# 52 early gathers, from 24 missing node tiles on, in a two-layer graph attention kernel on one Trainium2 core

## The chip, the cores and the metric

The kernel runs on one core of one Trainium2 chip. The metric is device time in microseconds. Times of engines come from one profiled execution, in which PE is the matrix engine, PEld its weight loads, DVE the vector engine, ACT the scalar engine, POOL the GpSimd engine and SP the engine that issues most plain DMAs. A gather (an indirect DMA: 128 rows of a table in DRAM, picked by 128 indices) is issued by POOL.

## The reference

A graph has N = 6250 nodes with 768 features and E = 100000 edges, sorted by destination, and each node has an edge to itself besides. The reference normalises the features, runs two layers of graph attention and two dense layers, and adds the input. For one attention layer:

```python
h = (x @ W).reshape(n, heads, -1)                  # layer 1: 4 heads of 64; layer 2: 1 head of 256
alpha_s = (h * a_src[None]).sum(-1)
alpha_d = (h * a_dst[None]).sum(-1)
e = jax.nn.leaky_relu(alpha_s[src] + alpha_d[dst], NEG_SLOPE)
m = jax.ops.segment_max(e, dst, num_segments=n)
e = jnp.exp(e - m[dst])
denom = jax.ops.segment_sum(e, dst, num_segments=n)
alpha = e / (denom[dst] + 1e-16)
out = jax.ops.segment_sum(h[src] * alpha[:, :, None], dst, num_segments=n)
return out.reshape(n, -1) + bias
```

The whole is `h = relu(layernorm(x))`, then `relu(gat)` twice, then `relu(h @ Wm1 + bm1) @ Wm2 + bm2`, added to `x`.

## The kernel before

Nodes are worked in NT = 49 tiles of 128, edges in tiles of 128 too. Two edge tiles are a pair, four are a group, and there are NG = 196 groups; a node tile corresponds to four groups in the loop (`t, j = divmod(g, 4)`). A row of layer 1's table holds 268 numbers: 4 heads of 64 features and a one, and 8 exponentials of the source scores.

The node phase (the loop over `i` in NT before L545) loads `x` and its transpose, normalises, multiplies by `W1` on PE, writes row tile `i` to `kept[i]` in SBUF, which stays there, and stores it in `table1` in DRAM (`store1`, L465). Then `layer_edges` runs for layer 1 and again for layer 2. For each group `g` it gathers the source rows of group `g + 8` (`gather`, issued at L641), turns the pairs of group `g` into weighted rows on DVE (`pair`, L708 to L720), and sums them over destinations by a product with a one-hot matrix on PE (`o_ps`, L732). Every second group the sums are taken up (`acc`, L753) and, once a node tile is complete, `node.steps` normalises it, turns it (`tp`, L884) and multiplies by the next weights (`h_ps`, L935). In layer 1 this makes `table2`, in layer 2 the output.

An ordinary gather of layer 1 needs the whole of `table1`. Some pairs are gathered early instead, in the node phase, from the part of the table that is there. `SOON` (L52) lists for each such pair how many node tiles are stored by then (NT minus the number that is missing). Its parts:

- `soon_places` (L331): for each index, whether it lies in the stored part (`soon_ok`), and the index times that (`soon_i`).
- `soon_rows(there)` (L337): called after the store of tile `there - 1`; gathers both tiles of each pair whose time this is, on POOL (L343), into a buffer of the ring `G` (pool `gathered`, 20 buffers of one pair, taken in turn).
- `soon_away` (L347): writes pairs from `G` to DRAM (`soon_d`, on SP, L351), which frees the buffer. In the node phase it does this for pairs that lie `SOON_HELD = 6` tiles back; at the start of layer 1 (L782) for the rest, in the order of their index.
- `soon_back` (L353): when the group's gather would be due, loads the pair from `soon_d` into a new buffer.
- `soon_sources` (L358) and `soon_hits` (L364): spread the pair's source indices over partitions and compare them on DVE with the numbers of the missing nodes, one 128x128 block for each missing tile (L370). The block matrix `soon_hit` has one buffer.
- `soon_missing` (L375): on PE, one product of such a block with `kept[T]` for each missing tile (L380; two records for each). Its PSUM tile shares two buffers with `tp` and `h_ps`.
- `soon_whole` (L383): on DVE, `row * soon_ok + missing` (L387), which completes the rows in `G`.

`SOON_AT` gives pair `i` the place of the second pair of group 8i + 11. One half-pair `k` is completed for each node tile `t`: hits at group 4k, product at 4k + 2, sum at 4k + 5. The order on each engine is that of the program, written out by hand (`manual_schedule`)[...].

Layer 2 has a smaller device of the same sort (`first_rows`, L321, 11 gathers), which is not changed.

Of the kernel before, what the change touches and what calls it, by code (L numbers as in the profile page):

```python
# [27 lines left out]
NT = -(-N // P)  # L28
# [20 lines left out]
THERE = {layer: [there for n, there in stages for _ in range(n)] for layer, stages in EARLY.items()}  # L49


SOON = [NT - m for m in (11, 20, 2, 19, 11, 18, 3, 17, 4, 16, 4, 15, 5, 15, 6, 14, 7, 13, 8, 12, 9, 18,  # L52
                         10)]
SOON_AT = {2 * (8 * i + 11) + 1: i for i in range(len(SOON))}
SOON_FROM, SOON_HELD = min(SOON), 6
BARE = 8


# [2 lines left out]
def kernel(  # L61
# [21 lines left out]
    nc = tc.nc  # L83
# [260 lines left out]
                        out=soon_G[i][:, t], out_offset=None, in_=table[1][:there * P],  # L344
                        in_offset=bass.IndirectOffsetOnAxis(ap=soon_i[:, i, t:t + 1], axis=0))

    def soon_away(there):  # L347

        for i in sorted(soon_G):
            if SOON[i] <= there:  # L350
                nc.sync.dma_start(soon_d[i], soon_G.pop(i).rearrange("p t c -> p (t c)"))  # L351

    def soon_back(i):  # L353
        G = rows_in(1)
# [3 lines left out]
    def soon_sources(pool, i):  # L358

        if i < len(SOON):  # L360
            soon_of[i] = pool.tile([P, 2 * P], I32, name="soon_of", bufs=2)
            nc.sync.dma_start(soon_of[i], bcast(src_rows, 2 * P, 2 * P * soon_pair[i]))

    def soon_hits(pool, k):  # L364

        i, t = divmod(k, 2)
        if i < len(SOON):
            m = NT - SOON[i]
            soon_hit[k] = pool.tile([P, NT - SOON_FROM, P], F32, name="soon_hit")
            nc.vector.tensor_tensor(  # L370
                soon_hit[k][:, :m],
                soon_of[i][:, t * P:(t + 1) * P].unsqueeze(1).to_broadcast([P, m, P]),
                nid_ps[:, SOON[i]:].unsqueeze(2).to_broadcast([P, m, P]), ALU.is_equal)

    def soon_missing(k):  # L375
        if 0 <= k < 2 * len(SOON):
            there, hit = SOON[k // 2], soon_hit.pop(k)
            soon_p[k] = ps.tile([P, TW[1]], F32, name="missing1", tag="n")
            for T in range(there, NT):
                nc.tensor.matmul(soon_p[k], hit[:, T - there], kept[T], start=(T == there),  # L380
                                 stop=(T == NT - 1))

    def soon_whole(G, k):  # L383
        if 0 <= k < 2 * len(SOON):
            i, t = divmod(k, 2)
            row = G[soon_pair[i]][:, t]
            nc.vector.scalar_tensor_tensor(row, row, soon_ok[:, i, t:t + 1], soon_p.pop(k),  # L387
                                           ALU.mult, ALU.add)
# [3 lines left out]
    with tc.tile_pool(name="w1p", bufs=1) as wp, tc.tile_pool(name="x1", bufs=6) as xp, \  # L392
# [107 lines left out]
        for i in range(NT):  # L500
            h = features1(i)
            if i == 0:
                centre(1)
                moments(2)
            elif i == 1:
                centre(2)
                moments(3)
                spread_means(3)
                moments(4)
            else:  # L510
                if i + 3 < NT:
                    moments(i + 3)
                if i + 2 < NT:
                    spread_means(i + 2)
                if i + 1 < NT:
                    centre(i + 1)
            if i == 0:
                fetch_x(6)
                fetch_x(7)
            if i + 8 < NT:  # L520
                fetch_x(i + 8)
            if i + 5 < NT:
                fetch_xT(i + 5)
            if i == 40:
                first_places()
            if 2 <= i < 2 + KI // 2:
                for k in range(2 * i - 4, 2 * i - 2):
                    nc.vector.tensor_reduce(w1[:, k, HID:], score_w[k], AX.X, ALU.add)
            if BARE <= i < 2 * BARE:
                scores1(i - BARE)  # L530
            keep1(i, *h)
            if 4 <= i < BARE + 4:
                halves[i - 4] = halve(heads_row(kept[i - 4])[:, :, :HID // 4])
            if BARE < i <= 2 * BARE:
                store1(i - BARE - 1)
            if BARE < i <= SOON_FROM - 3:
                store1(i - 1)
            if i >= SOON_FROM - 3:
                store1(i)
                soon_rows(i + 1)  # L540
                soon_away(i + 1 - SOON_HELD)
            if i >= 10:
                next(pieces, None)


# [69 lines left out]
    def layer_edges(layer, H, node, pre, matched, pre_pool):  # L615
# [4 lines left out]
        with tc.tile_pool(name=f"eg{layer}", bufs=5) as eg, \  # L620
# [157 lines left out]
            if layer == 1:  # L778
                for r in range(3):
                    fetch_rows(r)  # L780
                soon_sources(pre_pool, 0)
                soon_away(NT)  # L782
                fetch_rows(3)
                for u in range(4):
                    make_mask(u)
# [33 lines left out]
            for g in range(NG):  # L819
                t, j = divmod(g, 4)  # L820
                if layer == 2 and g >= NG - 2:
                    if g == NG - 2:
                        last_pairs()
                    continue
                if g == NG - 2:
                    at_end.append(g)
                gather(g + AHEAD)
                pair(g, 0)
                if g == NG - 1:
                    pair(g, 1)  # L830
                if g == NG - 2:
                    gather_up(NU - 2)
                advance(g)
                if g <= NG - 4:
                    make_hot(g + 1)
                if g in (NG - 4, NG - 3):
                    make_hot(g + 2)
                if j == 0:
                    if layer == 1:
                        fetch_rows(t + 4)  # L840
                        if t % 2:
                            soon_sources(pre_pool, (t + 1) // 2)
                    node.prefetch(t)
                    meet(t + 1)
                    if layer == 1:
                        soon_hits(pre_pool, t)
                elif j == (2 if t < NT - 1 else 1):
                    node.ahead(t)
                    if layer == 1:
                        soon_missing(t)  # L850
                elif j % 2:
                    if layer == 1 and j == 1:
                        soon_whole(G, t - 1)
                    make_mask((g + 7) // 2)
                if g == NG - 3:
                    idle_ps.append(ps.tile([P, 4 * P], F32, name="idle_ps", tag="e"))
                if g >= NG - 3:
                    stay_warm(3)
                if g < NG - 1:
                    pair(g, 1)  # L860
                advance(g)
                if j == 3:
                    join(t + 1)
                if taken_up(g) is not None:
                    gather_up(taken_up(g))
                if NG - 3 <= g < NG - 1:
                    stay_warm(3)
                hot.pop(g, None)
                if layer == 1 and g == NG - 6:
                    first_sources(2)  # L870
# [533 lines left out]
```

## Time and profile before

| | |
|---|---|
| median of 3 runs | 2589.47 us (2586.82 to 2594.48) |
| the profiled execution | 2102.47 us, of which the span is 2100.7 us |
| busy share of the span | PE 80%, PEld 58%, DVE 67%, ACT 20%, POOL 73% |
| mean granted clock of PE | 0.884 |
| gathers | 1507 at L641, 46 at L343, 11 at L321 |
| products of the missing rows (L380) | 1028 records, 249.1 us of PE |
| their one-hot rows (L370) | 46, 75.3 us of DVE |
| writes to `soon_d` | 23 of 268.0 KB, 6.9 us to landing in the median |
| loads from `soon_d` | 23 of 268.0 KB, 4.0 us |

The profiled execution is 487 us shorter than the median of the runs; the page gives no reason. A line of the page's groups reads: line, engine, operation, output from input, count, busy time, mean in ns of one, and the idle time just before them with what ended it. POOL's busy time does not hold the time in which it issues; PE's ends are modelled.

Three stages follow one another: the node phase to about 165 us, layer 1 to about 1097 us, layer 2 to the end. The stages differ in what fills them, so shares over the whole span say little.

### The profile page before, as it was taken

To read this page: it belongs to the slowest core of one execution; us is meant where nothing else is said; L and a number is where in the kernel's file an instruction comes from. 1 tells how busy PE (TensorE), PEld (TensorE's weight loads), DVE (VectorE), ACT (ScalarE), POOL (GpSimd) and SP (SyncE) were. 2 spreads that over 40 slices of the span, in tenths; PEclk is the share of its full clock that TensorE was granted. 3 is DMA by queue.
4 is the path that set the end of the run, shared out by engine and by line. 5 is a ranking of instruction groups with operands and counts; after the bars stand their busy time and mean duration, and the time that the engine had idled before them with its cause. 6 is when DMAs were issued, how large, how long until landed. Compare 5 with 4: busy or idle time off the path is not lost. (4 is left out here: it accounts for less than half of the span.)

```text
span 2100.7 us, 26499 instructions
## 1 busy us (share of the span) xinstructions
PE 1673.7 (80%) x7728; PEld 1215.5 (58%) x7729; DVE 1411.3 (67%) x4195; ACT 409.8 (20%) x1273; POOL 1523.7 (73%) x1666
## 2 busy tenths in 40 slices
PE   8986879877888888888878777777778777777787
PEld 6864657656665666666645545545455454554554
DVE  7856888878888787888866655555555555555554
ACT  5751111111111111111111111111111111111121
POOL 7057777777777777777777777777777777777774
PEclk9997999989988999999988788888888888888889
DMA  9998666666666666666557455555555555656554
GB/s 343 349 360 290 176 186 181 184 182 186 186 176 183 188 185 178 185 183 187 163 140 225 131 182 170 169 181 160 178 181 158 182 170 168 182 156 182 180 153 123
DMA packets 167328, 400.37 MB, mean 191 GB/s; under 512 B 36631, under 2 KB 54254, under 8 KB 167174
## 3 DMA queue, kind: packets, MB, share of 16 engines
q0 software_dynamic: 75072, 211.10, 38.6%
q1 hardware_dynamic: 90732, 185.99, 24.9%
q10 hardware_dynamic: 1370, 1.48, 0.3%
q8 instruction: 65, 1.06, 0.2%
q14 instruction: 89, 0.73, 0.1%
HBM read 333.87 MB, written 64.56 MB: 190 GB/s over the span
## 5 line engine op out<-in xcount | busy, mean ns | idle before, releaser
L641 POOL DMA_INDIRECT G<-table,src_i x1507 | 1431.2, 950 | 459.7 <-issue 334.5
L732 PE MATMUL o_ps<-G,hw 128*128 128x258 f32 x1564 | 468.9, 438 | 227.3 <-DVE hw L715 226.6
L732 PE MATMUL o_ps<-hw,hot 128*128 128x260 f32 x1564 | 456.7, 434 | 160.4 <-DVE hw L720 135.8
L732 PEld LDWEIGHTS o_ps<-G,hw 128*128 128x128 f32 x1564 | 320.7, 217 | 347.8 <-DVE hw L715 278.5
L708 DVE TENSOR_TENSOR e_ps<-G,e_ps 128x8 f32<-128x8 f32 (+1 forms) x782 | 129.1, 165 | 521.5 <-DMA G<-table,src_i 518.2
L732 PEld LDWEIGHTS o_ps<-hw,hot 128*128 128x128 f32 x1564 | 308.7, 209 | 278.7 <-DVE hw L720 197.6
L762 ACT ACTIVATE sum<-acc 32x260 f32<-32x260 f32 (+1 forms) x384 | 160.0, 417 | 1397.6 <-DVE acc L753 1336.9
L715 DVE TENSOR_SCALAR hw<-iota_ps,dcol,w 128x128 f32<-128x128 f32 x782 | 284.9, 406 | 14.5
L720 DVE TENSOR_TENSOR hw<-G,e_ps 128x520 f32<-128x520 f32 x391 | 271.8, 695 | 13.4
L380 PE MATMUL missing<-kept,soon_hit 128*128 128x268 f32 x1028 | 249.1, 400 | 0.0
L380 PEld LDWEIGHTS missing<-kept,soon_hit 128*128 128x128 f32 x1028 | 199.7, 198 | 36.6
L1058 PE MATMUL y_ps<-wm,mT 128*128 128x384 f32 x392 | 203.3, 654 | 0.3 <-ACT mT L1053 0.3
L438 PE MATMUL h_ps<-w,r 128*128 128x264 f32 (+1 forms) x588 | 139.5, 391 | 11.4 <-ACT r L428 11.2
L669 DVE TENSOR_TENSOR hot<-iota_ps,dcol 128x512 f32<-128x512 f32 x196 | 133.4, 681 | 0.0
L438 PEld LDWEIGHTS h_ps<-w,r 128*128 128x128 f32 x588 | 108.8, 192 | 34.8 <-ACT r L428 15.8
L1058 PEld LDWEIGHTS y_ps<-wm,mT 128*128 128x128 f32 x392 | 86.5, 245 | 64.7 <-issue 39.8
L343 POOL DMA_INDIRECT G<-table,soon_i x46 | 44.1, 960 | 81.0 <-DMA xTt<-in_xT 54.3
L753 DVE SCALAR_TENSOR_TENSOR acc<-acc,keep,o_ps 128x260 f32<-128x260 f32 (+1 forms) x192 | 91.2, 475 | 0.3 <-PE o_ps L732 0.3
L370 DVE TENSOR_TENSOR soon_hit<-soon_of,iota_ps 128x1408 f32<-128x1408 int32 (+18 forms) x46 | 75.3, 1636 | 14.8 <-PE missing L380 14.6
L718 DVE TENSOR_TENSOR e_ps<-e_ps,G 128x8 f32<-128x8 f32 x391 | 68.2, 174 | 13.6 <-DVE e_ps L708 0.2
L711 DVE TENSOR_TENSOR w<-e_ps,G 128x2 f32<-128x2 f32 x391 | 62.3, 159 | 14.3 <-DVE e_ps L708 1.1
L426 DVE TENSOR_TENSOR cent<-xTt,mean_ps 128x768 f32<-128x768 f32 x49 | 46.5, 949 | 33.6 <-DMA xTt<-in_xT 15.8
(415 smaller groups left out, 1172.5 us busy)
## 6 DMA issues: line engine op xcount, KB each, us to landing
xt<-in_x SPq DMA_DIRECT2D x96, 384.0 KB, 6.5
drow<-dmod_d SPq DMA_DIRECT2D x49, 512.0 KB, 5.8
mask_d<-mask SPq DMA_DIRECT2D x97, 256.0 KB, 2.2
mask<-mask_d SPq DMA_DIRECT2D x97, 256.0 KB, 4.4
G<-table,src_i POOLq DMA_INDIRECT x1507, 3.3
xTt<-in_xT SPq DMA_DIRECT2D x49, 384.0 KB, 7.6
out<-y SPq DMA_DIRECT2D x48, 384.0 KB, 3.3
table<-kept SPq DMA_DIRECT2D x49, 134.0 KB, 5.3
```

The source lines that it names most:

```text
L370: nc.vector.tensor_tensor(soon_hit[k][:, :m], soon_of[i][:, t * P:(t + 1) * P].unsqueeze(1).to_broadcast([P, m, P]), nid_ps[:, SOON[i]:].u ...
L380: nc.tensor.matmul(soon_p[k], hit[:, T - there], kept[T], start=(T == there), stop=(T == NT - 1))
L438: nc.tensor.matmul(h_ps[:, :n], r[:, k], w1[:, k, :n], start=(k == 0), stop=(k == KI - 1))
L641: nc.gpsimd.indirect_dma_start(out=G[k // 2][:, k % 2], out_offset=None, in_=table[layer], in_offset=bass.IndirectOffsetOnAxis(ap=src_i[:, ...
L669: nc.vector.tensor_tensor(hot[g][:, T[0]:T[0] + n], iota_ps.unsqueeze(1).to_broadcast([P, n, P]), dcol[:, k:k + n].unsqueeze(2).to_broadca ...
L708: nc.vector.tensor_mul(v, e2, rho)
L715: nc.vector.tensor_scalar(hw[:, t], iota_ps, dcol[:, k:k + 1], w[:, t], ALU.is_equal, ALU.mult)
L720: nc.vector.tensor_mul(hw, Gp[:, :, :RW[1]].rearrange("p t (h c) -> p t h c", h=H), w.unsqueeze(3).to_broadcast([P, 2, H, C + 1]))
L732: nc.tensor.matmul(o_ps[u], l, r[:, :RW[layer]], start=(g % 2 == 0 and k == 0), stop=(g % 2 == 1 and k == tiles(g)[-1]))
L753: nc.vector.scalar_tensor_tensor(acc, run[0], keep[:, u % 2:u % 2 + 1], o_ps.pop(u), ALU.mult, ALU.add)
L762: nc.scalar.activation(done[t][r], acc[r], AF.Copy)
L1058: nc.tensor.matmul(y_ps, mT[:, j], wm2[:, j, s * half:(s + 1) * half], start=False, stop=(j == KH - 1))
```

## The change

The list of early pairs has 26 entries instead of 23, up to 24 tiles missing instead of 20; the sum of the missing tiles goes from 257 to 334, for each of a pair's two tiles. Pairs sit at every seventh group from 11 on (`SOON_GROUP`), the last at 186. Up to 16 pairs stay in the ring `G`; `soon_away` writes the oldest beyond that, and at the start of layer 1 all 16, oldest first. The half-pairs of the pair at group `at` are completed at fixed distances from it: hits at `at - 10` and `at - 6`, products at `at - 8` and `at - 5`, sums at `at - 6` and `at - 3`, and the sources are loaded at `at - 13`. The chain of preparations (`pieces`) starts at node tile 8 instead of 10. `soon_hit` grows with its 24 blocks by 2 KB a partition, and `dynamic_dma_scratch_size` goes from 8192 to 4096.

```diff
-SOON = [NT - m for m in (11, 20, 2, 19, 11, 18, 3, 17, 4, 16, 4, 15, 5, 15, 6, 14, 7, 13, 8, 12, 9, 18,
-                         10)]
-SOON_AT = {2 * (8 * i + 11) + 1: i for i in range(len(SOON))}
-SOON_FROM, SOON_HELD = min(SOON), 6
+SOON = [NT - m for m in (14, 24, 2, 23, 3, 22, 4, 21, 5, 20, 6, 19, 6, 18, 7, 18, 8, 17, 9, 16, 10, 15, 11,
+                         13, 11, 12)]
+SOON_GROUP = [7 * i + 11 for i in range(len(SOON))]
+SOON_AT = {2 * g + 1: i for i, g in enumerate(SOON_GROUP)}
+SOON_FROM, SOON_HELD = min(SOON), 16
...
-    def soon_away(there):
-
-        for i in sorted(soon_G):
-            if SOON[i] <= there:
-                nc.sync.dma_start(soon_d[i], soon_G.pop(i).rearrange("p t c -> p (t c)"))
+    def soon_away(held):
+
+        for i in list(soon_G)[:max(len(soon_G) - held, 0)]:
+            nc.sync.dma_start(soon_d[i], soon_G.pop(i).rearrange("p t c -> p (t c)"))
...
-                soon_away(i + 1 - SOON_HELD)
-            if i >= 10:
+                soon_away(SOON_HELD)
+            if i >= 8:
                 next(pieces, None)
...
-                soon_away(NT)
+                soon_away(0)
...
                     if layer == 1:
                         fetch_rows(t + 4)
-                        if t % 2:
-                            soon_sources(pre_pool, (t + 1) // 2)
                     node.prefetch(t)
                     meet(t + 1)
-                    if layer == 1:
-                        soon_hits(pre_pool, t)
                 elif j == (2 if t < NT - 1 else 1):
                     node.ahead(t)
-                    if layer == 1:
-                        soon_missing(t)
                 elif j % 2:
-                    if layer == 1 and j == 1:
-                        soon_whole(G, t - 1)
                     make_mask((g + 7) // 2)
+                if layer == 1:
+                    for i, at in enumerate(SOON_GROUP):
+                        for k, hits_at in ((2 * i, at - 10), (2 * i + 1, at - 6)):
+                            if g == hits_at + 3 + (k % 2 == 0):
+                                soon_whole(G, k)
+                            if g == hits_at:
+                                soon_hits(pre_pool, k)
+                            if g == hits_at + 1 + (k % 2 == 0):
+                                soon_missing(k)
+                        if g == at - 13:
+                            soon_sources(pre_pool, i)
...
-                   dynamic_dma_scratch_size=8192)
+                   dynamic_dma_scratch_size=4096)
```

## The prediction

> **What bounds the kernel now.** I read the page first, then the list of waits, then tables of stages, then the timeline around the two places that the change touches. In the page, the costliest group is POOL's gather, and its idle time has no releaser but its own issue:
>
> ```profile
> L641 POOL DMA_INDIRECT G<-table,src_i x1507 | 1431.2, 950 | 459.7 <-issue 334.5
> ...
> L343 POOL DMA_INDIRECT G<-table,soon_i x46 | 44.1, 960 | 81.0 <-DMA xTt<-in_xT 54.3
> ```
>
> 950 ns of work and some 0.30 us of issue make 1.25 us a gather. The table of stages shows the same number of gathers, 80 in 100 us, in layer 1 (first line) and in layer 2 (second), whatever PE and DVE do beside them:
>
> ```profile
> 600.00:700.00 100.00, 83.75 (x388) 63.72 (x388) 81.63 (x213) 14.41 (x53) 75.80 (x80) 0.89 0.65 183
> ...
> 1500.00:1600.00 100.00, 76.23 (x342) 51.06 (x341) 53.02 (x194) 17.12 (x45) 75.79 (x80) 0.84 0.58 172
> 0.00:165.00 165.00, 147.85 (x657) 117.77 (x658) 114.17 (x279) 104.93 (x340) 76.45 (x143) 0.99 1.00 349
> ```
>
> The columns are PE, PEld, DVE, ACT, POOL, clock, DMA share, GB/s. The third line is the node phase: its DMA share is 1.00, so bytes set its length. From the list of waits, two lines matter:
>
> ```profile
> DVE e_ps L708 <- DMA G<-table,src_i: 518.2, 381, 5.2
> ...
> DVE soon_hit L370 <- PE missing L380: 14.6, 12, 2.0
> ```
>
> DVE waits for gathers 518 us (128.5 of them in layer 1), so the consumers stand behind POOL. The timeline at the border of the two phases:
>
> ```profile
> 170.63 0.94 POOL L343 DMA_INDIRECT G<-table,soon_i  x1 [0.30 <-issue]
> 171.88 0.95 POOL L641 DMA_INDIRECT G<-table,src_i  x1 [0.30 <-issue]
> ...
> 164.67 0.32 SPq L465 DMA_DIRECT2D table<-kept  x1
> ...
> 176.74 2.74 SPq L351 DMA_DIRECT2D soon_d<-G  x5
> ```
>
> POOL runs without a pause from 154.23 us to its last gather at 2077.10, but for 1.5 us at the border of the layers (L321 waits for `kept` L940). The last node tile's store is issued at 164.67, and the first ordinary gather starts the moment the last early one is out. So the end is: start of the unbroken stream, plus gathers times pitch, plus a tail of 24 us (2077 to 2101). The chain of waits agrees: from 1112 us on it alternates between `DMA G<-table,src_i` and what consumes those rows.
>
> [...] 0.95 us of record, 3.3 us to landing in the median. [...] 0.92 granted in layer 1, 0.84 in layer 2 where PE idles more, and near 1 within the long bursts.
>
> **The change, part by part.**
>
> *Fewer gathers in the stream.* 23 pairs become 26, so 46 early gathers become 52 and layer 1's own fall from 736 to 730. From 171.88 to 1097.58 us there were 736, or 1.258 us each. Six fewer: -7.5 us. This is the one large term.
>
> *Node phase.* The six gathers go here. One is 128 rows of 1072 B, 137 KB, together +0.82 MB. In return pairs stay in SBUF: before, 18 of 23 were written to `soon_d` during the phase and 5 at 176.74; now 10 of 26. The start of layer 1's stream hangs on when the backlog of early gathers begins: the last seven pairs (there = 42 and up) ran in one piece from 154.23, after a wait on `table<-kept`. The new list has seven pairs from there on too (7, 6, 6, 5, 4, 3, 2 for 7, 6, 5, 4, 4, 3, 2). Up to that tile there are 4 writes instead of 10 (-1.65 MB) and 6 more gathers. By share of the engines for a MB a gather costs 1.37 times a write (38.6% for 211.10 MB against 24.9% for 185.99 MB), so the sum is -1.65 + 1.13 = -0.52 MB, at 349 GB/s -1.5 us; by plain bytes it is -2.4. I take -2. Bounds: -4 (all bytes of the phase count) and +1 (gathers that begin three to four tiles earlier delay loads of x). POOL has the room: a pair needs 2.5 us and tiles come about 2.8 to 3.4 us apart.
>
> *Border.* SP now issues 16 writes of 268 KB instead of 5 (3.0 MB more). They go oldest first, where the old order put the pair with two missing tiles in front, so all five waited for its landing at 176.74. Now only the last waits so. Behind it on SP stand `drow` row 3 and four mask stores; the masks of the first groups need rows 0 to 2, issued before. The first ordinary gathers find four buffers free of the 20 (ages 6 to 9, already written), good for 8 gathers or 10 us, and then want one more each 2.5 us, while the writes land at about 0.8 us each. Cost taken: 0; bound +3 if the extra bytes hold up the first rows, which layer 1's lag can swallow.
>
> *Missing rows.* The sum of missing tiles goes from 257 to 334 a half-pair, 514 to 668 in all. In the window 205 to 1105 us the 503 tiles recorded took PE 243.5 us, 0.484 us each: +74.5 us. DVE's one-hot rows took 75.3 us for 514, 0.146 each: +22.6, and six more `G` mends of 0.483 us: +2.9. In that window PE was busy 746 of 900 us and DVE 729, so both fit: 821 and 755 of about 892. What hides them is time in which PE and DVE wait for gathers. If that cover is gone, the first rival below gives the price.
>
> *Spacing.* This is tight. Seven groups of gathers take 26 x 1.25 = 32.5 us. The heaviest burst before shows what follows:
>
> ```profile
> 230.52 9.20 PE L380 MATMUL missing<-kept,soon_hit 128*128 128x268 f32 x40
> 239.55 3.67 PE L732 MATMUL o_ps<-hw,hot 128*128 128x260 f32 x16
> ...
> 249.96 9.20 PE L380 MATMUL missing<-kept,soon_hit 128*128 128x268 f32 x40
> ...
> 239.75 2.82 DVE L370 TENSOR_TENSOR soon_hit<-soon_of,iota_ps 128x2560 f32<-128x2560 int32 x1 [1.77 <-PE missing L380]
> ```
>
> A tile takes 0.46 us here, four groups of other PE work about 9.2, and DVE is blocked (1.77 us) until the first product is done, since `soon_hit` has one buffer. A pair of 24 costs 11.0 us a half. Its two products now stand three groups apart, then four: 11.0 + 6.9 + 1.6 of gaps = 19.5 us for a supply of 13.9; then 11.0 + 9.2 + 1 = 21.2 for 18.6. The lag grows to some 8 us. The light pair after it (2 tiles) runs at DVE's own 3.5 us a group, 24.5 for 32.5, and gives 8 us back. So consumers and POOL break even over 14 groups in the first third; later pairs (10 and 15, 11 and 12) have room. POOL feels a lag only when its ring of 20 buffers is full, ten groups or 46 us ahead, less about 10 for rows in flight and in work: 35 us of cushion. A lag of 8 to 20 us costs nothing.
>
> *New waits.* `soon_whole` follows its product after two groups, not three; behind it on DVE stand that group's pair products, on which PE's `o_ps` waits. The old rule for `soon_hit` had the same two groups, so no new limit. Loads of kept pairs rise by three: 0.8 MB beside a DMA share of 0.65.
>
> [...] Halved scratch. [...] with 6.4 us to landing in the node phase and a pitch of 1.25, five gathers were in flight, so half holds at least 2.5, and layer 1 has 3.3 / 1.25 = 2.6. I take 0; the bad end is the third rival.
>
> Sum: -7.5 - 2 = -9.5 us, 2102.47 to 2093.0. The median of the runs, 2589.47, is 1.2316 times the profiled time, and the page does not say why. If every duration is stretched alike, the gain is 11.7; if a constant 487 us is added, 9.5; if only gathers are slower (487 / 1564 = 0.31 us each), 6 x 1.57 + 2 = 11.4. I take 11.5: 2578.0.
>
> **Rivals.** First, slower: PE and DVE become the bound of layer 1. Against: the balance above[...]. For: PE at 821 of 892 us leaves 71 us, and before it lost 154 to waits. If half of those waits (77 us) don't close, the need is 898, about equal; if three quarters don't (116), it is 937, 45 over. Past the cushion the lag shows at the border of layer 2, whose first gathers need `table2`: +45 - 9.5 = +35 in the profile at worst; halfway, +20, or 2614 after stretching. It decides from a lag over 35 us inside the layer, or any lag left at group 186. A PE that is slower in the timed runs than in the profile would bring it on.
>
> Second, no change to be seen: the node phase gives nothing or loses a us, and only some 6 to 7.5 us of gathers remain, 2582 to 2584. For: landing times there are 5 to 9 us and irregular.
>
> Third, the scratch doesn't do what it says at no cost: with two gathers in flight the pitch is 3.3 / 2 = 1.65 us, +0.40 x 1558 = +623 us, 3200 or more. It decides if POOL shows waits with no releaser over 0.3 us.
>
> **How the numbers follow.** A measurement of this kernel can tell 0.3%, 7.8 us, from no change. Forecast 0.54, all of it faster; second 0.20, the same; first 0.23 and third 0.03, slower. The forecast's own range is 2566 to 2581. Taking in the second rival and most of the first, up to a lag that costs 35 us net of cushion, gives 2564 to 2612.
>
> **What would show it.** POOL at 80 gathers in 100 us through layer 1, the first L641 gather near 170 us, 730 of them in the layer, PE busy some 0.92 there, DVE's wait for gathers in layer 1 down from 128 us to well under 100. Wrong: POOL waiting for `o_ps` or `hw` for more than its issue time, a DVE that waits for `missing` for over 100 us in all, or a pitch above 1.27.

## The result, and the profile after

The changed kernel takes 2680.41 us (median of 4 runs, 2668.17 to 2686.14), against 2591.33 us before (4 runs, 2586.82 to 2594.48): a ratio of 1.0327 [1.0296, 1.0359]. It is slower by 89 us, where 11.5 us faster was forecast.

One fact has to stand ahead of everything else, since no number below can be read without it. The executions of this case are of two kinds. In one, the kernel before takes 2102 to 2106 us, in the other 2583 to 2591 us, and nothing in between was seen. Kernels that were run together, as one set, showed one kind throughout; six sets of experiments fell three and three. The profile before, on which the prediction rests, is of the first kind (2102.47 us). The times of the result, and the trace of the changed kernel, are of the second. I call them the 2100 kind and the 2590 kind; what the change costs is compared within a kind only. What sets the kind is not known. The number of the chip doesn't tell it: number 1 stands beside one set of the first kind (2105.81 us for the kernel before) and two of the second (2582.72 and 2586.72 us). The last section has signs that the recording of the traces has to do with it.

The groups of the changed kernel's page (2590 kind; the last number of a line is the idle time before the group's instructions and what ended it):

```profile
L641 POOL DMA_INDIRECT G<-table,src_i x1501 | 1432.6, 954 | 964.9 <-issue 371.8
...
L380 PE MATMUL missing<-kept,soon_hit 128*128 128x268 f32 x1336 | 356.9, 416 | 98.1 <-issue 96.6
...
L387 DVE SCALAR_TENSOR_TENSOR G<-G,soon_ok,missing 128x268 f32<-128x268 f32 x52 | 25.6, 492 | 347.4 <-remote 218.8
```

A gather still takes 0.95 us, but POOL's idle time ahead of gathers is 964.9 us, and only 371.8 of it is its own issue. The 52 short mends on DVE (L387, the sum that completes a half-pair; 25.6 us of work) have 347.4 us of waiting ahead of them. 100 us of layer 1 (us, PE, PEld, DVE, ACT, POOL, clock, DMA share, GB/s), first in the changed kernel, then in the kernel before in a later execution of the 2590 kind:

```profile
600.00:700.00 100.00, 72.27 (x332) 54.40 (x330) 58.99 (x150) 9.55 (x36) 57.06 (x60) 0.87 0.49 143
600.00:700.00 100.00, 70.98 (x329) 53.59 (x328) 64.45 (x165) 10.84 (x40) 56.91 (x60) 0.83 0.48 138
```

Both have 60 gathers in 100 us, where the profile before had 80: that is the kind, and not the change. No engine is near full in the changed kernel: PE is busy 72 of 100 us, DVE 59. So no engine's work alone bounds this stage; the engines wait, for the most part for each other. The list of waits over the whole span says for whom (us in total, times, longest):

```profile
PE o_ps L732 <- issue: 284.0, 266, 2.7
...
DVE G L387 <- remote: 218.8, 27, 8.9
...
POOL G L641 <- DVE hw L720: 163.8, 55, 8.7
...
PE o_ps L732 <- DVE hw L720: 130.4, 47, 11.5
...
POOL G L641 <- DVE e_ps L708: 107.8, 25, 11.9
DVE G L387 <- PE missing L380: 98.0, 13, 12.9
PE missing L380 <- issue: 96.6, 74, 2.9
```

POOL waits for DVE, DVE for PE, and PE for DVE or for nothing that the profile shows ("issue"). In the profile before, PE had one single wait of this last kind, 4.5 us. The label is to be read with care here. A trace of the 2590 kind holds some 12,000 to 14,000 semaphore events, one of the 2100 kind 41,000 to 42,000, so a wait whose event is missing comes out as "issue" too. Of the 482.1 us that PE has in all in the changed kernel, 222 stand before instructions that have no semaphore to wait for; for these "issue" is sure. What they look like is seen in PE's timeline, in the first product of layer 1 (14 missing tiles, two records each; start, duration, number of records, idle time ahead):

```profile
210.71 0.61 PE L380 MATMUL missing<-kept,soon_hit 128*128 128x268 f32 x1 [2.22 <-issue]
213.50 0.60 PE L380 MATMUL missing<-kept,soon_hit 128*128 128x268 f32 x1 [2.18 <-issue]
216.30 0.60 PE L380 MATMUL missing<-kept,soon_hit 128*128 128x268 f32 x1 [2.20 <-issue]
219.13 0.61 PE L380 MATMUL missing<-kept,soon_hit 128*128 128x268 f32 x1 [2.23 <-issue]
...
262.52 4.21 PE L380 MATMUL missing<-kept,soon_hit 128*128 128x268 f32 x8 [1.29 <-issue]
```

In the middle of one product, with nothing to wait for, a record comes only every 2.1 to 3.5 us; its 28 records take 56 us, where the same kernel's take 6.5 us in the 2100 kind (below). This first stall is the longest. Later ones are shorter: a half of 46 records takes 18.65 us from 388.13 on, and the pair's other half, undisturbed, 10.55 us.

The second sign of the 2590 kind is a PE that is done, while DVE doesn't hear of it. PE's timeline around a light product (two tiles, four records):

```profile
364.67 1.15 PE L380 MATMUL missing<-kept,soon_hit 128*128 128x268 f32 x4
365.65 3.67 PE L732 MATMUL o_ps<-hw,hot 128*128 128x260 f32 x16
369.16 0.38 PE L887 MATMUL tp<-ident,o 128*128 128x128 f32 x2
381.04 4.64 PE L732 MATMUL o_ps<-hw,hot 128*128 128x260 f32 x12 [11.50 <-DVE hw L720]
```

and DVE's timeline of the same stretch:

```profile
376.34 0.49 DVE L387 SCALAR_TENSOR_TENSOR G<-G,soon_ok,missing 128x268 f32<-128x268 f32 x1 [7.46 <-remote]
376.75 3.21 DVE L370 TENSOR_TENSOR soon_hit<-soon_of,iota_ps 128x2944 f32<-128x2944 int32 x1
```

The product's records end at 365.82, the mend that reads it starts at 376.34. "Remote" means that an event ended the wait and that no instruction or transfer near it in time was found to have sent it. Here it is an event of PE's own semaphore, at 376.32 us, which comes long after the product's last record; so it is for all 27 "remote" waits of the mends. For 11.5 us PE has no `hw` to work on, because DVE, which makes `hw`, stands at the mend (7.5 us) and then at the next hits (3.2 us). Each completed half-pair is a meeting of PE and DVE, and here a meeting can cost both some 8 to 11 us.

### The profile page after: what moved, and what is told of

It reads as the page before. It is cut to its first block, busy times and chain, and to the rows that moved or that the text cites. A ratio compares the mean times of both kernels' runs of the same rounds, so it can differ in the third digit from the quotient of the medians.

```text
span 2666.3 us, 27201 instructions
## 1 busy us (share of the span) xinstructions
PE 1877.1 (70%) x8035; PEld 1353.8 (51%) x8037; DVE 1417.2 (53%) x4213; ACT 411.4 (15%) x1273; POOL 1530.4 (57%) x1666
## 3 DMA queue, kind: packets, MB, share of 16 engines
q8 instruction: 68, 1.11, 0.2%
## 4 chain that ended last, share of the span: by engine, by line
PE 36%; DVE 21%; issue 20%; another core or an unknown queue 15%; DMA 3%; POOL 2%; ACT 2%; DVEq 0%; SPq 0%; ACTq 0%; POOLq 0%
PE o_ps L732 18%; PE missing L380 7%; PE y_ps L1061 4%; DVE hw L720 3%; DVE hot L669 3%; DVE soon_hit L370 3%; PE h_ps L438 3%; POOL G L641 2%; DVE e_ps L718 2%; DVE e_ps L708 2%; DMA G<-table,src_i 2%; DVE hw L715 2%; DVE acc L753 2%; PE tp L1051 1%
## 5 line engine op out<-in xcount | busy, mean ns | idle before, releaser
L641 POOL DMA_INDIRECT G<-table,src_i x1501 | 1432.6, 954 | 964.9 <-issue 371.8
L732 PE MATMUL o_ps<-G,hw 128*128 128x258 f32 x1564 | 532.5, 470 | 261.9 <-issue 183.5
L732 PE MATMUL o_ps<-hw,hot 128*128 128x260 f32 x1564 | 487.7, 453 | 243.3 <-DVE hw L720 130.4
L732 PEld LDWEIGHTS o_ps<-G,hw 128*128 128x128 f32 x1564 | 358.7, 235 | 410.6 <-issue 280.7
L732 PEld LDWEIGHTS o_ps<-hw,hot 128*128 128x128 f32 x1564 | 335.1, 223 | 358.2 <-DVE hw L720 152.7
L380 PE MATMUL missing<-kept,soon_hit 128*128 128x268 f32 x1336 | 356.9, 416 | 98.1 <-issue 96.6
L380 PEld LDWEIGHTS missing<-kept,soon_hit 128*128 128x128 f32 x1336 | 268.2, 203 | 175.6 <-issue 128.3
L720 DVE TENSOR_TENSOR hw<-G,e_ps 128x520 f32<-128x520 f32 x391 | 271.8, 695 | 22.2 <-DVE e_ps L718 5.3
L387 DVE SCALAR_TENSOR_TENSOR G<-G,soon_ok,missing 128x268 f32<-128x268 f32 x52 | 25.6, 492 | 347.4 <-remote 218.8
L1065 DVE TENSOR_TENSOR y<-y_ps,xt 128x384 f32<-128x384 f32 (+1 forms) x98 | 54.6, 557 | 272.5 <-PE o_ps L732 90.9
L1056 ACT ACTIVATE mT<-tp,bm1c 128x128 f32<-128x128 f32 x98 | 30.7, 364 | 534.5 <-PE o_ps L732 260.9
L687 PE MATMUL e_ps<-win,mask 128*128 128x12 bf16 (+1 forms) x1564 | 63.5, 167 | 54.2 <-issue 47.7
L370 DVE TENSOR_TENSOR soon_hit<-soon_of,iota_ps 128x768 f32<-128x768 int32 (+22 forms) x52 | 96.7, 1860 | 0.0
```

What stands on the lines that cost most here:

```text
L370: nc.vector.tensor_tensor(soon_hit[k][:, :m], soon_of[i][:, t * P:(t + 1) * P].unsqueeze(1).to_broadcast([P, m, P]), nid_ps[:, SOON[i]:].u ...
L641: nc.gpsimd.indirect_dma_start(out=G[k // 2][:, k % 2], out_offset=None, in_=table[layer], in_offset=bass.IndirectOffsetOnAxis(ap=src_i[:, ...
L720: nc.vector.tensor_mul(hw, Gp[:, :, :RW[1]].rearrange("p t (h c) -> p t h c", h=H), w.unsqueeze(3).to_broadcast([P, 2, H, C + 1]))
L732: nc.tensor.matmul(o_ps[u], l, r[:, :RW[layer]], start=(g % 2 == 0 and k == 0), stop=(g % 2 == 1 and k == tiles(g)[-1]))
```

## The experiments

The theories of the change's cost are three. The prediction's: POOL's pitch is the bound and products are hidden. S (so named in the expectations): PE is short of instructions, so that each product lengthens layer 1. And C: it is the meetings of PE and DVE, which the expectations lay at first to the new distances and later to the density of the pairs. The scratch (theory R), the held pairs and the new distances are tried apart from these. I give layer 1 below as the time from the last early gather to the first gather of layer 2; for the 2590 kind it is 1214.1 us in an unaltered kernel before, run again, and 1295.7 in the changed one, +81.6. These are single executions, and thirty runs of the kernel before in one set lie between 2578.79 and 2599.65 us, so a difference of some 10 us between two of them says little. Layer 2 is no part of the question: 1178 to 1187 us in the 2590 kind in every kernel, about 992 in the 2100 kind.

**The scratch alone.** The kernel before, with the one line changed:

```diff
-                   dynamic_dma_scratch_size=8192)
+                   dynamic_dma_scratch_size=4096)
```

> The kernel before with the scratch of the software DMAs at 4096 instead of 8192 and nothing else. Theory S (PE is starved of instructions in an ordinary run, and the added products are what costs): no change, 2591 us within 8, and a profile with PE idle for 'issue' by some hundreds of us, as in the changed kernel, not the 2100 us of the first profile. Theory R (the halved scratch is the cost): most of the 89 us, 2650 to 2680 us.

1.0002 [0.9993, 1.0011] (2100 kind). The halved scratch costs nothing there, and the third rival falls. In the 2590 kind it wasn't run by itself, but it is in two kernels below that are faster than before.

**The products cut.** The changed kernel, with one product for each half-pair instead of one for each missing tile: 52 for 668.

```diff
-            for T in range(there, NT):
-                nc.tensor.matmul(soon_p[k], hit[:, T - there], kept[T], start=(T == there),
-                                 stop=(T == NT - 1))
+            for T in range(there, there + 1):
+                nc.tensor.matmul(soon_p[k], hit[:, T - there], kept[T], start=True, stop=True)
```

> The changed kernel with one product for each half-pair instead of one for each missing tile, 52 instead of 668; it leaves out the other missing rows of the early pairs, all else stays. Theory S: 154 products more cost 89 us, 0.58 us each, so 616 fewer bring 2680 down by up to 356 us, to 2320 to 2400, less where gathers then bind. Theory R: 2660 to 2680. Theory C (the tight waits between DVE and PE at the new distances cost): the waits for products vanish, 2590 or a little less, but not far below before.

> The changed kernel with 52 products instead of 668, as in products_cut (it leaves out the other missing rows), to have it beside the changed kernel. If the kernel before takes 2102 here: 2097 again, so that the 616 products are worth only what after_again is above that. If it takes 2591: theory S 2320 to 2400, theory C about 2590.

> The changed kernel with 52 products (it leaves out the other missing rows). Where before takes 2590: theory S 2290 to 2350, as light_list_2 or below it; theory C 2560 to 2600. Where before takes 2102: 2097 again.

All three fell in the 2100 kind: 0.9977 [0.9967, 0.9988], 0.9977 [0.9967, 0.9987], 0.9978 [0.9968, 0.9989]. These figures mean little without the next run, which ran in the same set as the second.

**The changed kernel again**, nothing altered.

> The changed kernel unaltered, beside the kernel before on the same chip. The kernel before took 2102 us in forty runs of the first batch and 2591 us in the runs of the result, so the first thing to be told is which of the two this chip gives. If 2102: theory S (instructions come late in the runs of the result, and only there do products cost) expects what the prediction summed for the profile, 2093, and theory C (tight waits between DVE and PE) 2120 to 2170, 3% as in the result. If 2591: 2680 again by both.

0.9977 [0.9969, 0.9985]: 2100.57 us against 2105.27. In the 2100 kind the change makes the kernel faster, and by as much with 668 products as with 52. There, the products cost nothing that these runs can tell. The groups of this run's page, in the form of those above:

```profile
L641 POOL DMA_INDIRECT G<-table,src_i x1501 | 1430.8, 953 | 457.6 <-issue 329.9
...
L380 PE MATMUL missing<-kept,soon_hit 128*128 128x268 f32 x1336 | 314.4, 393 | 0.0
```

100 us of its layer 1:

```profile
600.00:700.00 100.00, 86.61 (x427) 68.21 (x425) 84.85 (x211) 13.57 (x50) 75.91 (x80) 0.95 0.66 183
```

DVE's waits in its layer 1:

```profile
DVE e_ps L708 <- DMA G<-table,src_i: 80.4, 76, 3.8
DVE G L387 <- PE missing L380: 33.8, 14, 4.1
```

and the product of 14 tiles that PE did record by record above:

```profile
192.85 6.49 PE L380 MATMUL missing<-kept,soon_hit 128*128 128x268 f32 x28
```

80 gathers in 100 us, no idle time ahead of the products, DVE waiting for gathers 80 us, and 33.9 us of idle time ahead of the mends where the other kind has 347.4. The code is the same; what differs is that PE does not stand still within a product and that its signals arrive in time.

**The old list.** The changed kernel with before's 23 pairs, eight groups apart. The held pairs, the new distances and the scratch stay as changed.

```diff
-SOON = [NT - m for m in (14, 24, 2, 23, 3, 22, 4, 21, 5, 20, 6, 19, 6, 18, 7, 18, 8, 17, 9, 16, 10, 15, 11,
-                         13, 11, 12)]
-SOON_GROUP = [7 * i + 11 for i in range(len(SOON))]
+SOON = [NT - m for m in (11, 20, 2, 19, 11, 18, 3, 17, 4, 16, 4, 15, 5, 15, 6, 14, 7, 13, 8, 12, 9, 18,
+                         10)]
+SOON_GROUP = [8 * i + 11 for i in range(len(SOON))]
```

> The changed kernel with the list of before, 23 pairs and 514 products, at every eighth group; hold of 16, distances of completion and scratch as changed. Theory S: 2591 within 15. Theory C: the distances remain, so 2620 to 2670. Theory R: 2650 to 2680.

> Old list and spacing of eight groups, with hold, distances and scratch as changed. Where before takes 2590: theory S 2575 to 2595; theory C, if the distances cost, 2630 to 2680. Where before takes 2102: 2100 again.

> Where before takes 2590: if the distances and the hold cost, 2640 as dense_257 (+50 to 60 us); if the denser pairs cost, within 15 us of before. Where before takes 2102: 2100 again.

0.9991 [0.9984, 0.9998] and 0.9993 [0.9986, 1.0] in the 2100 kind, 0.9961 [0.9946, 0.9976] in the 2590 kind. Layer 1 in the third is 1203.8 us, 10 less than before. So the held pairs, the distances and the scratch together do no harm, which is a miss for C in its first form (2620 to 2680 us), and the harm is in the list: in its products, its density, or both.

**A light list.** Seven pairs with few missing tiles, far apart: 14 early gathers, 70 products.

```diff
-SOON = [NT - m for m in (14, 24, 2, 23, 3, 22, 4, 21, 5, 20, 6, 19, 6, 18, 7, 18, 8, 17, 9, 16, 10, 15, 11,
-                         13, 11, 12)]
-SOON_GROUP = [7 * i + 11 for i in range(len(SOON))]
+SOON = [NT - m for m in (8, 2, 7, 3, 6, 4, 5)]
+SOON_GROUP = [25 * i + 18 for i in range(len(SOON))]
```

> The changed kernel with 7 early pairs only, of 2 to 8 missing tiles, at every 25th group: 14 early gathers instead of 52 and 70 products instead of 668. Theory S: 444 products fewer than before are worth up to 257 us, and 32 gathers more cost little while PE is the bound: 2350 to 2450. If gathers bind, as the prediction had it: 32 gathers at 1.25 us more than before, about 2630.

> The 7 early pairs of light_list (70 products, 14 early gathers). Where before takes 2590: theory S 444 products fewer at 0.58 to 0.66 us each, 2300 to 2350; theory C (only distances or density cost) 2560 to 2600. Where before takes 2102: 2128 again.

> Where before takes 2590: 444 products fewer at 0.24 us, the price from before_plus_154, are 107 us, and the waits between DVE and PE at the products go as well (DVE stood 368 us there in before_plus_154): 2350 to 2480. Where before takes 2102: 2130 again.

In the 2100 kind 1.0123 [1.0103, 1.0142] and 1.0123 [1.0106, 1.0139]: 26 us slower. 32 gathers more in layer 1 are 40 us at 1.258 us each, and the first ordinary gather starts 14 us sooner (157.95 for 171.88); POOL's pitch explains it. In the 2590 kind 0.9859 [0.982, 0.9898]: 37 us faster, 2549.83 us. The same edit has opposite signs in the two kinds. A larger gain was expected, 2350 to 2480 us: a miss, since most of PE's stalls don't go with the products that are taken away. It still has 203.6 us of them ahead of `o_ps` in layer 1.

**PE made the bound on purpose.** To see what the change costs when PE is the limit, layer 1's products with the masks (L687) were issued 17 times over in before, in the changed kernel and in the light list.

```diff
-                    for k in range(a, b):
+                    for k in list(range(a, b)) * (17 if layer == 1 else 1):
```

> The kernel before with layer 1's 16 small products of each node tile (e_ps, L687) issued 17 times over, same values, so that PE gets 0.55 x 16 = 8.8 us more for each 4 groups and becomes the bound of layer 1. PE then needs about 10.5 + 4.8 + 8.8 = 24.1 us for 4 groups where gathers give 18.8: some 260 us longer than the kernel before, 2360 where that takes 2102. By itself it only sets the stage. If this chip is one on which the kernel before takes 2590, more than 2850.

> The changed kernel with the same load. Theory S (where PE is the bound, for whatever reason, the 154 products more are on the path and the six gathers fewer are not): 154 x 0.46 = 71 us, less 3.5 of the node phase, so 60 to 75 us longer than loaded_before. Theory C (the distances of completion cost, not the products): far more than 75 us. The prediction's own reading (gathers bind whatever PE does): 5 us shorter.

> The list of 7 early pairs with the same load: 444 products fewer than loaded_before, 204 us at 0.46, and 32 gathers more that now have cover. Theory S: 150 to 200 us shorter than loaded_before, the sign opposite to light_list's +26 us. If gathers bound still: longer.

This set fell in the 2590 kind: 3237.88, 3262.19 and 2943.66 us, or 1.2496 [1.2449, 1.2543], 1.2596 [1.2549, 1.2643] and 1.1368 [1.1324, 1.1412] of before. Under an equal load the changed kernel is 24 us longer than before, and the light one 294 us shorter. From light to before there are 444 products, 0.66 us each; from before to the changed kernel 154, only 0.16 each. One price for a product doesn't fit both, and S as stated fails; so does C, which had put far more than 75 us on the changed kernel. PE's own account shows why no single price fits. In layer 1 its busy time rises from before to the changed kernel by 73 us (1184.2 to 1257.7), which is 0.48 us a product, while its waits labelled "issue" shrink. The runs show that products can be on the path, not what they cost in the unloaded kernel.

**The kernel before, run again** unaltered, for the noise and for traces that can stand beside those of the other kernels. The two runs fell one in each kind.

> The kernel before, unaltered, for its trace on a chip where it takes 2590 us. Theory S: PE idle for 'issue' (no releaser) by 400 to 700 us over the span, against 4.5 us in the first profile, in both layers; POOL's gathers wait for buffers. If the chip is of the 2102 us kind: the first profile again.

> Where before takes 2590: PE's waits without a releaser 200 to 300 us in layer 1, its waits for hw about 40 us as in before_plus_154 and not 130 as in dense_257, layer 2 from the last L321 gather to the end 1183 us. Where before takes 2102: the first profile again.

1.0 [0.9991, 1.0008] in the 2100 kind, 0.999 [0.9974, 1.0006] in the 2590 kind. The second gives the waits of the kernel before in layer 1 where the result was measured:

```profile
DVE soon_hit L370 <- remote: 206.8, 26, 10.7
...
PE o_ps L732 <- issue: 143.2, 146, 8.6
...
DVE soon_hit L370 <- PE o_ps L732: 79.7, 10, 10.4
PE o_ps L732 <- DVE hw L720: 57.8, 49, 3.3
```

The stalls of PE and the late signals are there before the change already. What the change more than doubles is the last line, PE's wait for `hw`: 57.8 us to 130.4. POOL's wait for `hw`, 18.2 us here and 163.8 in the changed kernel, is no sign of the harm: the old list has 141.8 us of it, in a kernel that is faster than before. Nor are DVE's waits at the meetings by themselves. Ahead of hits and mends together they are 325 us here, 246 with the old list and 347 in the changed kernel.

PE's work over the stage of layer 1 tells the rest, here (first line) and in the changed kernel:

```profile
172.00:1390.00 1218.00, 841.90 (x3648) 617.02 (x3650) 754.51 (x1945) 134.13 (x476) 703.20 (x741) 0.80 0.49 142
172.00:1470.00 1298.00, 909.81 (x3968) 684.57 (x3968) 773.49 (x1959) 135.83 (x481) 700.11 (x734) 0.82 0.46 135
```

The stage is 80 us longer. PE works 68 us more and waits 73 us more for `hw`, while its waits labelled "issue" in this stage shrink by 48 us, from 282 to 234; smaller waits, 13 us less in sum, are the rest. The next two runs take the two growing terms apart.

**The products alone, and the density alone.** The kernel before, with 152 products added: for each half-pair the first three tenths of its products are issued once more ahead of the real ones, which overwrite them.

```diff
         def soon_missing(k):
...
+            for T in range(there, there + round(0.3 * (NT - there))):
+                nc.tensor.matmul(soon_p[k], hit[:, T - there], kept[T], start=True, stop=True)
             for T in range(there, NT):
```

> The kernel before with 152 products more and nothing else: three tenths of each half-pair's products are issued once more ahead of its sum, into the same PSUM tile, and overwritten. Where before takes 2590: theory S 70 to 100 us more, 2660 to 2690; theory C (spacing and distances) within 10 of before. Where before takes 2102: theory S none, within 3 us, as the cover of 154 us of idle PE holds.

Beside it the changed kernel with 26 pairs, seven groups apart, but with before's 514 products:

```diff
-SOON = [NT - m for m in (14, 24, 2, 23, 3, 22, 4, 21, 5, 20, 6, 19, 6, 18, 7, 18, 8, 17, 9, 16, 10, 15, 11,
-                         13, 11, 12)]
+SOON = [NT - m for m in (11, 16, 2, 17, 3, 16, 4, 16, 5, 15, 5, 14, 6, 14, 6, 13, 7, 13, 7, 12, 8, 11, 8, 10, 9, 9)]
```

> The changed kernel with its 26 pairs at every seventh group, its distances, hold and scratch, but fewer missing tiles, 257 for a half-pair as before (514 products; 2 to 17 missing). Where before takes 2590: theory S 2575 to 2600; theory C 2640 to 2680. Where before takes 2102: six gathers fewer and nothing else, 2095 to 2098, not slower than after_again's ratio of 0.9977.

Both fell in the 2590 kind: 2618.11 us, 1.0151 [1.012, 1.0182], for the products alone; 2640.78 us, 1.0224 [1.0199, 1.0248], for the density alone. The first misses both forecasts, S's 2660 to 2690 and C's "within 10 of before". The second is at the edge of C's 2640 to 2680, far from S's 2575 to 2600. "Density" here means the whole of what 26 pairs at every seventh group bring: 52 meetings for 46, closer together, and six early gathers more. Layer 1 is 1242.5 us in the first (+28.4 against before) and 1248.9 in the second (+45.1 against the old list's 1203.8, which has the same products and everything else of the change). The second also starts layer 1 some 18 us later, whose likely cause is that its list puts nine pairs on the last seven node tiles where the others put seven; that is its own, and isn't in the 45 us. The stage of layer 1 in the old list (third run):

```profile
172.00:1378.00 1206.00, 836.57 (x3653) 621.52 (x3653) 749.57 (x1947) 136.19 (x477) 703.91 (x739) 0.79 0.51 145
```

and in the dense list:

```profile
193.00:1442.00 1249.00, 833.28 (x3658) 624.22 (x3658) 753.57 (x1960) 135.93 (x478) 697.89 (x732) 0.79 0.49 140
```

PE and DVE do the same work to within 4 us, at the same clock, and the stage is 43 us longer. It is all waiting. Whose, the waits in layer 1 of the old list show:

```profile
PE o_ps L732 <- issue: 150.2, 125, 2.9
...
PE o_ps L732 <- DVE hw L720: 44.2, 41, 5.9
```

against those of the dense list, whose line numbers are lower by one:

```profile
DVE G L386 <- remote: 239.9, 31, 8.9
...
PE o_ps L731 <- issue: 144.8, 131, 8.3
...
PE o_ps L731 <- DVE hw L719: 132.1, 38, 10.8
```

PE's own stalls don't grow (150.2 and 144.8 us ahead of `o_ps`); its wait for `hw` triples, from 44.2 to 132.1 us, with DVE held at the mends longer (246.2 us of idle time ahead of them in the old list, 304.2 here). In the run with products alone it is the other way round. That wait is 42.1 us, less than before, and PE's "issue" waits in layer 1 come to 259 us, again less than before's 282, while its busy time rises from 841.9 to 906.9 us. So the products cost PE's own time, and the density costs waits for `hw`. That it is the meetings which make these waits is read from the lists; no run removes a meeting and leaves the rest.

The sum in layer 1: old list -10, density +45, products +28, together +63 of the 81.6 us. By the medians of the runs, each against the kernel before in its own set, it is -8, +48 (58 - (-8), less the 18 us ahead of layer 1) and +35, together 75 of 89 us. The 14 to 19 us that are left may belong to both together, or to heavier products in tighter places, or be the spread between executions; no run takes them apart. The node phase doesn't enter: in the changed kernel the last early gather starts at 174.95 us, 1.9 sooner than in before.

Of the versions run in both kinds, the old list with the rest of the change is the only one that is not slower than before in either (0.9991 and 0.9993, 0.9961). In the 2100 kind the changed kernel is still ahead of it (0.9977), and in the 2590 kind the light list is, at 0.9859; but each of these two loses in the other kind.

## Why the prediction was wrong

**What failed** is the step from the profile to the runs: "The median of the runs, 2589.47, is 1.2316 times the profiled time, and the page does not say why. If every duration is stretched alike, the gain is 11.7". I took a gap of 487 us for a stretch of the same schedule. It was another schedule. Nothing of POOL's work is stretched (950 ns a gather in the kernel before in both kinds); PE stalls and signals late, and with that the bound of layer 1 passes from POOL to the chain of PE and DVE. A sum made of POOL's pitch has no force there. On that chain the change adds 68 us of PE's work and 73 us of waits for `hw` to layer 1, two terms that the prediction put at nothing, and it came out 89 us slower instead of 11.5 us faster.

**Fewer gathers** (-7.5): not on the path of the 2590 kind. In the 2100 kind layer 1 went from 927.0 us (170.63 to 1097.58) to 922.4 (166.93 to 1089.35), -4.6; the kernel before, run again, has 929.4, which makes it -7.0. The term was right there within what two executions tell.

**Node phase** (-2): -1.9 us by the last early gather in the 2590 kind. In the 2100 kind the border moved by 3.7 us against the profile before and by 1.1 against its repeat (168.0), within the bounds:

```profile
166.93 0.95 POOL L344 DMA_INDIRECT G<-table,soon_i  x1 [0.30 <-issue]
168.18 0.95 POOL L641 DMA_INDIRECT G<-table,src_i  x1 [0.31 <-issue]
```

The border, too, cost nothing there: the first ordinary gather follows the last early one at the pitch. In the 2590 kind the changed kernel loses 2.6 us at that place, and the kernel before lost 3.5.

**Missing rows** (+74.5 us of PE, hidden): right in the 2100 kind, where cutting 616 products changed nothing, and wrong in the 2590 kind, where 152 cost 28 us of layer 1 (35 by the medians). The cover named for them, PE's and DVE's waits for gathers, is not seen there: by the list of waits DVE waits for gathers 1.1 us in the changed kernel's layer 1. All three signs that the prediction gave for its being wrong came true in that kind: POOL waits for `hw` beyond its issue time, DVE waits for `missing` 98.0 us by name and 218.8 "remote", and the pitch in layer 1 is 1.77 us (730 gathers in 1291.9 us). They tell of the kind more than of the change: the kernel before has a pitch of 1.64 us there.

**Spacing and new waits** (0): right in the 2100 kind, wrong in the other, and this is the largest term, 45 us. The balance of supply and need left out what a meeting costs when the signal comes late.

**Scratch** (0): right in the 2100 kind, where it was run by itself (1.0002). How many gathers in flight the scratch allows was an estimate; no run shows a limit.

**The sum on its own kind**: -9.5 forecast, -4.7 measured (0.9977), so about half, and the right way. The profiled run of the changed kernel also ends 28.5 us after its last gather, not 24, with four products (L732) near the end at 2.09 us that had taken 1.03 us some 5 us before.

**The first rival** named the mechanism, PE and DVE as the bound, and its trigger: "A PE that is slower in the timed runs than in the profile would bring it on." Its price of 2614 was too low, since it was made from waits that fail to close and not from meetings. The gap of 487 us was evidence for it, and was in hand when the 0.23 was given.

**Still open**: what makes an execution one of the 2590 kind, whether the kernel has that kind at all when nothing is recorded, and the 14 to 19 us that no run splits.

## What to carry to other kernels

A timed median that lies far from the profiled time can mean, as here with 2589.47 against 2102.47 us, that the profile shows another schedule than the one that is timed; until the gap has a cause, a forecast needs both schedules as cases of about equal weight. Work that hides in waits in one of them may lie on the path in the other: here 616 products fewer left the ratio at 0.9977 in one, and 152 more cost 28 us of layer 1 in the other. So look at what a change adds per meeting of two engines, and not at busy time alone. Of two versions that were equal in work here, the one with fewer meetings, further apart, was the safer, by 45 us of layer 1. And before a wait is read from a trace, count whether the trace still holds its events: 12,806 in the changed kernel's of the 2590 kind, 41,868 in the first profile of the kernel before.

## What the runs showed of the hardware

The same program ran at 2102 and at 2591 us. POOL's gathers (950 ns) and DVE's operations (L720: 695 ns) have the same durations in both. PE is busy 1673.7 us at a mean granted clock of 0.884 in the first, 1816.0 us at 0.798 in the second, and its waits for nothing that the profile shows come to 4.1 us in the kernel before, run again, of the 2100 kind and 551.5 in that of the 2590 kind (482.1 in the changed kernel).

These stalls come in episodes. Counting idle times over 0.25 us labelled "issue", less than 12 us apart as one, the two traces of the changed kernel have:

```
kind   matmul records   episodes   records per episode
2590   8035             78         103
2100   8036             0          -
```

An obvious suspect is the supply of instructions. The page lists 68 packets, 1.11 MB, on the instruction queue q8, in both kinds: 16 KB each, and 236 matmul and weight-load records of PE for each packet. Of the 222 us that PE stands still before instructions without a semaphore, in the changed kernel of the 2590 kind, 2.5 fall while one of the 68 packets is in flight. The packets are in flight for 2.7% of the span, so even chance would give more, 6.0 us. That episodes and packets are about as many (78 and 68) looks like coincidence: in these traces PE's stalls don't wait for a packet.

Another suspect is the recording itself. Three things in the traces point to it. In the first 100 us both kinds hold about the same number of semaphore events (2137 and 2172 in the changed kernel's two traces), and PE has no wait labelled "issue". From then on the events of the 2590 kind fall to about 4 a microsecond in the mean, against about 20 in the other, and the stalls before instructions without a semaphore begin at 203 us. While PE stands there, from 204 to 262 us, the trace holds 81 events, one for each 0.7 us. And PE's records then start 2.1, 2.8 or 3.5 us apart (the timeline of the first product above), which are multiples of that same 0.7. So what slows the recording and what slows PE keep step, and the same thing could delay PE's signals. Whether one causes the other isn't shown: every run on record has a granted clock of its own and so was recorded. Until there is a run without recording, the 89 us hold for recorded executions of the 2590 kind, and the 4.7 us gained for those of the 2100 kind.
